# Four graph layers on one adjacency: VectorE's order in the attention layers written out, with small operations in lumps

## The chip, the cores and the metric

The kernel runs on one core of one Trainium2 chip. The metric is the device time of one execution in microseconds; a kernel's time is the median of its runs. All times below are microseconds.

## What is computed

A feature matrix x (4096 nodes, 64 features) passes through four layers over the same 0/1 adjacency matrix (4096 x 4096, float32). Each layer adds its result to x and normalizes the rows:

```python
x = _layernorm(x + _L0_gnn_ref(x, adj, L0_gnn_W, L0_gnn_b))
x = _layernorm(x + _L1_gnn_ref(x, adj, L1_gnn_r, L1_gnn_w_att, L1_gnn_b_att))
x = _layernorm(x + _L2_gnn_ref(x, adj, L2_gnn_weight, L2_gnn_bias))
x = _layernorm(x + _L3_gnn_ref(x, adj, L3_gnn_att_w, L3_gnn_att_b))
```

Layer 0 is a mean over neighbours, followed by a weight matrix, a relu and a normalization of rows. Layer 2 sums support rows (x times a weight matrix) over the last neighbours of a row, each weighted by a power of one half by its place in the row. Layers 1 and 3 are attention in hyperbolic space; their core is

```python
adj_att = sigmoid(left[:, None] + right[None, :] + b_att[0]) * adj
x_local = logmap(x[:, None, :], x[None, :, :], c)      # for every pair of nodes
support = einsum('ij,ijd->id', adj_att, x_local)
return proj(expmap(x, support, c), c)
```

where `left` and `right` are one number for each node. The pairwise `logmap` is not built as a 4096 x 4096 x 64 array: the kernel brings it to a function of one number z for each pair of nodes, and sums rows of features weighted by it.

## The kernel before, in words

**Staging.** The adjacency does not stay on the chip. Each layer streams it once, in 64 loads of 1 MB (`load`), into a pool of six buffers, all issued by the sync engine. The nodes on the output side form four groups of 1024 columns, taken in the order 3, 2, 1, 0 (`GROUPS`). For each group the 32 blocks of 128 source rows are taken two at a time, so that a layer has 4 x 16 = 64 pairs of blocks.

**An attention pass** (`attend`, L914 to L962). For each block of a pair, PE builds z (128 x 1024) in PSUM by three kinds of matmul (L935, L938, L941; z has two buffers), ScalarE (ACT) makes `sig`, the sigmoid (L943), and `sq`, a square of z (L946), and VectorE (DVE) makes t = max(z, 0) * sig (L949). After both blocks of the pair VectorE makes t = (sq + const) * t on 128 x 2048 (L951), and PE adds the pair to the sums `acc` of the group (L955). These three VectorE operations a pair, two L949 and one L951, are the large ones.

**The small work between.** When a group's pass is over, its sums are turned back to rows and go through `move` (L972 to L1072): about 90 VectorE operations, most on [128, 8] (one number for each of the group's 1024 nodes), a few on [128, 512] (all features of the group). It ends with the normalized rows of the next layer. `norm_rows` and `prepare` (with its part `second`) do the like for the rows that enter an attention: they build the operands of the z matmuls, and `left` and `right`. `linear` and `supports` make layer 2's support rows. The reciprocal square roots are `rsqrt` (L669): a first guess by integer arithmetic and three Newton steps (L677, L678, L679), each operation of which reads the one before it.

**What places the small work.** These parts are Python generators. `later` puts one into one of two queues, `tick(n)` advances a counter by n, and a queue's first generator runs to its next `yield` when its wait has passed; `yield n` asks for a wait of n ticks. `attend` calls `tick(rate)` behind each L949 and behind L951, where `rate` is given for each of the four groups. Three helpers give waits: `soon()`, `near()` and `after(small)`; `place[0]` says which layer runs. `need(tag)` ticks until a part is done.

**What sets the order on the engines.** The source gives one order; a scheduler then places instructions on each engine as it expects them to become ready. Layers 0 and 2 keep the source's order on PE and ACT (`FIXED`), and leave VectorE to the scheduler. In both attentions all engines are left to it. VectorE therefore often has one small operation between two large ones, whatever the source's order.

The functions that the change touches:

Of the kernel before, what the change touches and what calls it, by code (L numbers as in the profile page):

```python
# [21 lines left out]
D = 64  # L22
# [36 lines left out]
def gnn_stack_kernel(  # L59
# [509 lines left out]
    def stream(fits):  # L569

        with ExitStack() as st:
# [46 lines left out]
            def soon():  # L618


                return 0 if place[0] in (0, 2) else 1

            def after(small):


                each = {0: 1.6, 2: 6.0}.get(place[0])
                return 1 if each is None else 1 + int(small / each)

# [40 lines left out]
            def rsqrt(a, name):  # L669

                n = a.shape[1]
                r, t = nums(name, n), nums("rs_t", n)
                V.tensor_scalar(
                    r.bitcast(I32), a.bitcast(I32), -0.5, float(0x5F3759DF), ALU.mult, ALU.add
                )
                for _ in range(3):
                    V.tensor_mul(t, r, r)  # L677
                    V.scalar_tensor_tensor(t, t, -0.5, a, ALU.mult, ALU.mult)  # L678
                    V.scalar_tensor_tensor(r, t, 1.5, r, ALU.add, ALU.mult)  # L679
                return r  # L680

# [63 lines left out]
            def curved(c, name, least):  # L745


                c2, sc, rsc, of_y, root, short = (
                    num(keep, name + n, 1)
                    for n in ("_c2", "_sc", "_rsc", "_of_y", "_root", "_short")  # L750
                )
                V.tensor_scalar(c2, c, -2.0, None, ALU.mult)
                V.tensor_copy(rsc, rsqrt(c, "rsc"))
                V.tensor_mul(root, rsc, c)
                V.tensor_scalar(of_y, rsc, -((2.0 * UNIT) ** -0.5), None, ALU.mult)
                V.tensor_scalar(rsc, rsc, 0.996, None, ALU.mult)
                V.tensor_scalar(sc, root, -((2.0 * UNIT) ** 0.5), None, ALU.mult)
                V.tensor_scalar(short, root, least, None, ALU.mult)
                return c, c2, sc, rsc, of_y, root, short

            def norm_rows(layer, s, v, x2_to):

                m, v2, sq = nums("n_m"), nums("n_v2"), grp("sq")
                V.tensor_reduce(m, v, AX.X, ALU.add)
                V.tensor_scalar(m, m, 1.0 / D, None, ALU.mult)
                yield soon()
                V.tensor_sub(v, v, over(m))
                nc.gpsimd.tensor_mul(sq, v, v)
                yield soon()
                yield soon()  # L770
                V.tensor_reduce(v2, sq, AX.X, ALU.add)
                yield soon()
                V.tensor_scalar(m, v2, 1.0 / D, 1e-5, ALU.mult, ALU.add)
                r = rsqrt(m, "n_r")
                yield soon()
                V.tensor_mul(x_of(layer)[:, blocks(s), :], v, over(r))
                V.tensor_mul(x2_to, r, r)
                V.tensor_mul(x2_to, x2_to, v2)
                yield soon()

            def prepare(layer, s, att, b_att, curve, least, good, small):
# [6 lines left out]
                V.tensor_scalar(bg, cx2[:, at], -1.0, 1.0, ALU.mult, ALU.add)  # L788
                V.reciprocal(rbg, bg)

                V.tensor_scalar(rbg, rbg, -0.13, 0.0, ALU.max, ALU.min)
# [5 lines left out]
                def second():  # L797
# [12 lines left out]
                    for k, of in ((7, 0), (8, 0), (9, 1)):  # L810
                        nc.gpsimd.tensor_scalar(
                            ed[:, :, k], hl[:, :, of], -2.0 / UNIT, None, ALU.mult
                        )
                    V.tensor_sub(ys[:, :, D : 2 * D], y, ys[:, :, :D])

                    m, g, w = nums("m"), nums("g"), grp("xw")
                    V.tensor_scalar(g, cx2[:, at], 1.0, 1.0 / D, ALU.add, ALU.mult)
                    V.tensor_scalar(m, rbg, CUBE / UNIT, None, ALU.mult)
                    yield 1
                    V.tensor_add(w, xg, over(g))  # L820
                    yield 1
                    V.tensor_mul(xe[:, at, :], w, over(m))

                    q, q1, t = nums("q"), nums("q1"), nums("tt")
                    V.tensor_scalar(q, x2[:, at], least, c, ALU.max, ALU.mult)
                    V.tensor_scalar(q1, q, SMALL, None, ALU.max)
                    rt = rsqrt(q1, "rt")
                    V.tensor_mul(t, q1, rt)
# [32 lines left out]
                    V.tensor_scalar(m, bg, of_y, None, ALU.mult)  # L861
                    yield 1
                    lr, own = row.tile([P, WB, 2], F32, name="lr"), nums("own")
# [108 lines left out]
            def move(layer, s, sums, curve):  # L972
# [13 lines left out]
                held.pop()  # L986
                yield near()
                V.tensor_reduce(sum_1, of, AX.X, ALU.add)
# [5 lines left out]
                nc.scalar.activation(sq, u, AF.Square)  # L994
                yield near()
                yield soon()
                V.tensor_reduce(uu, sq, AX.X, ALU.add)
# [7 lines left out]
                V.tensor_mul(kx, k, x2g)  # L1005
                V.scalar_tensor_tensor(t2, d, -2.0, kx, ALU.mult, ALU.add)
                V.tensor_mul(t2, t2, k)
                V.tensor_add(t2, t2, uu)
# [5 lines left out]
                un, r_un = nums("un"), nums("r_un")  # L1014
                V.scalar_tensor_tensor(un, t2, root, rsqrt(t2, "r_t2"), ALU.mult, ALU.mult)
                V.tensor_scalar(un, un, fac, short, ALU.mult, ALU.max)
# [3 lines left out]
                nc.scalar.activation(th, un, AF.Tanh, scale=lam)  # L1020
                yield near()
                V.scalar_tensor_tensor(un, r_un, fac, th, ALU.mult, ALU.mult)
# [9 lines left out]
                V.tensor_add(y2, xy, y2)  # L1032
                V.tensor_add(den, den, xy)
                V.tensor_sub(p, y2, p)
                V.tensor_scalar(den, den, 1e-15, None, ALU.max)
# [8 lines left out]
                V.tensor_mul(t, q, q)  # L1044
                V.scalar_tensor_tensor(w2, qd, 2.0, px, ALU.mult, ALU.add)
                V.tensor_mul(t, t, uu)
                V.tensor_mul(w2, w2, p)
# [3 lines left out]
                yield soon()  # L1051
                n = rsqrt(t, "n")
                V.tensor_scalar(n, n, rsc, 1.0, ALU.mult, ALU.min)
# [8 lines left out]
                V.tensor_scalar(w2, w2, 1.0 / D, 1e-5, ALU.mult, ALU.add)  # L1062
                r = rsqrt(w2, "n")
                V.scalar_tensor_tensor(p, p, 1.0, r, ALU.add, ALU.mult)
# [3 lines left out]
                V.tensor_mul(u, u, over(q))  # L1068
                yield soon()
                yield soon()  # L1070
                V.tensor_add(x_of(layer + 1)[:, at, :], u, w)
                yield after(72)  # L1072

            def linear(layer, s, weights, finish):

                for h in range(2):
# [18 lines left out]
                    yield near()  # L1095
                    finish(slice(s * WB + h * SB, s * WB + (h + 1) * SB), t)
                    held.pop()
                    yield 1

            def supports(at, t):  # L1100

                nc.scalar.activation(halves[:, at, :D], t, AF.Copy, scale=SUP)
                V.scalar_tensor_tensor(
                    halves[:, at, D:], t, SUP, halves[:, at, :D], ALU.mult, ALU.subtract
                )
# [21 lines left out]
            with ExitStack() as lp:  # L1127
# [45 lines left out]
                def own_part(at, t):  # L1173

                    V.tensor_add(xw[:, at, :], t, b0_sb[:, None, :].to_broadcast([P, SB, D]))

                def end_0(s, tops):
# [3 lines left out]
                    for top, low in tops:  # L1181
                        t = take(F32, P, SB, P)
                        for k in range(SB):
                            cols = slice(k * P, (k + 1) * P)
                            to = t[:, k, : D + 1]
                            nc.tensor.matmul(to, top[:, cols], sum_w, start=True, stop=False)
                            nc.tensor.matmul(to, low[:, cols], count_w, start=False, stop=True)
                        ts.append(t)
                    for h, t in enumerate(ts):
                        at = slice(s * WB + h * SB, s * WB + (h + 1) * SB)  # L1190
# [4 lines left out]
                        V.tensor_add(zz, zz, xw[:, at, :])  # L1195
                    held.clear()
                    V.tensor_scalar(z, z, 0.0, None, ALU.max)
                    sq, n2 = grp("sq"), nums("n2")
                    nc.gpsimd.tensor_mul(sq, z, z)
                    yield 1  # L1200
                    V.tensor_reduce(n2, sq, AX.X, ALU.add)
                    V.tensor_scalar(n2, n2, 1e-24, None, ALU.max)
                    n = rsqrt(n2, "n")
                    yield 1
# [8 lines left out]
                with tc.manual_schedule(engines=FIXED):  # L1213
                    for s in GROUPS:
# [42 lines left out]
                        if s > 0:  # L1257
                            own_of = linear(0, s - 1, w0_sb[:D, :], own_part)
                            later(in_turn((0, s - 1), own_of))


# [19 lines left out]


            attention(1, curve1, (2, 1, 1, 1), lambda s: linear(2, s, w2_sb, supports))


            place[0] = 2

            def end_2(s, sums):
# [3 lines left out]
                t = to_rows_of(sums)  # L1292
                yield 1
                V.scalar_tensor_tensor(
# [84 lines left out]

            attention(3, curve3, (4, 1, 1, 1), store)  # L1380

# [84 lines left out]
```

## Time and profile before

| | us |
|---|---|
| median of 3 runs | 1155.24 (1150.9 to 1157.15) |
| profiled execution | 1151.7 |
| its span in the profile | 1150.0 |
| PE busy in the span | 1019.8 (89%) |
| VectorE busy in the span | 960.8 (84%) |
| ACT busy in the span | 812.2 (71%) |
| POOL busy in the span | 60.9 (5%) |

The layers follow one another; in the profiled execution layer 0 runs to 192.7, attention 1 to 528.4, layer 2 to 768.0, attention 3 to 1112.6, and the last group's move and the stores to 1150.0.

The rows of the profile for the attention's inner operations, both attentions together (busy us and mean ns of one, then idle time of the engine ahead of them and what ended most of it):

```
L943 ACT ACTIVATE sig<-left_b,right 128x1024 f32<-128x1024 f32 x256 | 293.8, 1149 | 44.8 <-DVE t L949 33.7
L949 DVE SCALAR_TENSOR_TENSOR t<-z,sig 128x1024 f32<-128x1024 f32 x256 | 309.8, 1215 | 15.5 <-ACT sq L946 14.6
L946 ACT ACTIVATE sq<-z,turn 128x1024 f32<-128x1024 f32 x256 | 281.4, 1105 | 30.2 <-PE z L941 27.9
L951 DVE SCALAR_TENSOR_TENSOR t<-sq,t 128x2048 f32<-128x2048 f32 x128 | 292.9, 2288 | 0.7
L955 PE MATMUL acc<-t,xe 128*64 128x512 f32 x1024 | 260.3, 622 | 33.5 <-DVE t L951 30.0
```

A matmul's duration includes the time that it overlaps with its neighbours, and so does that of a VectorE operation to a smaller part: the distance from one start to the next is what an operation takes on a busy engine.

### The profile page before, as it was taken

What the parts mean: (1) busy time and instruction counts of PE and PEld (TensorE: products, weight loads), DVE (VectorE), ACT (ScalarE), POOL (GpSimd) and SP (SyncE); (2) the same over time, 40 slices, a digit from 0 to 9 for tenths busy, and PEclk for the clock granted to TensorE, in tenths of its full rate; (3) what the DMA queues carried; (4) which work ended last, traced back from release to release, by engine and by line L of the source; (5) the groups of instructions that cost most, each with busy time, mean ns of one, the idle gap of its engine ahead of it and who ended that gap; (6) DMA issues with size and microseconds to landing.
All of it is one profiled execution on the core that took longest, in us unless ns stands there. A gap on an engine that the chain in (4) does not pass through costs nothing.

```text
span 1150.0 us, 13516 instructions
## 1 busy us (share of the span) xinstructions
PE 1019.8 (89%) x4917; PEld 389.6 (34%) x4917; DVE 960.8 (84%) x1901; ACT 812.2 (71%) x823; POOL 60.9 (5%) x97
## 2 busy tenths in 40 slices
PE   6889997899899999988999997998788999899970
PEld 3445554233333333332333232332323333233220
DVE  7587888989999899989773584249988999999996
ACT  0003215899889799976767688777997999889860
POOL 0020120000000000000000020001100000000001
PEclk9998998999999999999999999999998999999995
DMA  9999898546456455643988886695354655555400
GB/s 352 421 385 412 358 390 337 199 158 217 180 214 220 156 214 215 220 160 141 323 300 310 314 308 255 227 358 193 110 183 155 223 213 215 210 211 212 154 0 22
DMA packets 38418, 271.57 MB, mean 236 GB/s; under 512 B 4550, under 2 KB 4550, under 8 KB 5574
## 3 DMA queue, kind: packets, MB, share of 16 engines
q1 hardware_dynamic: 37440, 269.50, 63.0%
q10 hardware_dynamic: 902, 1.12, 0.3%
q8 instruction: 40, 0.66, 0.2%
q14 instruction: 36, 0.29, 0.1%
HBM read 269.55 MB, written 1.05 MB: 235 GB/s over the span
## 4 chain that ended last, share of the span: by engine, by line
DVE 54%; PE 30%; ACT 6%; DMA 5%; issue 2%; POOL 2%; ACTq 0%; POOLq 0%; SPq 0%; DVEq 0%
DVE t L951 21%; DVE t L949 21%; PE z L1340 9%; PE acc L1356 5%; PE acc L1229 5%; DMA edges<-in_adj_dram 5%; PE acc L955 3%; ACT sq L946 2%; ACT sq L1349 1%; PE aux L1092 1%; PE z L935 1%; PE aux L842 1%; ACT sig L943 1%; PE z L938 1%; DVE junk L741 1%
## 5 line engine op out<-in xcount | busy, mean ns | idle before, releaser
L943 ACT ACTIVATE sig<-left_b,right 128x1024 f32<-128x1024 f32 x256 | 293.8, 1149 | 44.8 <-DVE t L949 33.7
L949 DVE SCALAR_TENSOR_TENSOR t<-z,sig 128x1024 f32<-128x1024 f32 x256 | 309.8, 1215 | 15.5 <-ACT sq L946 14.6
L946 ACT ACTIVATE sq<-z,turn 128x1024 f32<-128x1024 f32 x256 | 281.4, 1105 | 30.2 <-PE z L941 27.9
L951 DVE SCALAR_TENSOR_TENSOR t<-sq,t 128x2048 f32<-128x2048 f32 x128 | 292.9, 2288 | 0.7
L955 PE MATMUL acc<-t,xe 128*64 128x512 f32 x1024 | 260.3, 622 | 33.5 <-DVE t L951 30.0
L935 PE MATMUL z<-edges,two_i 128*128 128x512 bf16 x512 | 202.7, 396 | 20.5 <-DVE t L949 20.3
L941 PE MATMUL z<-dst,src 74*128 74x512 f16 x512 | 196.2, 383 | 0.0
L938 PE MATMUL z<-lo_hi,hi_lo 128*128 128x512 f16 x512 | 195.4, 382 | 0.0
L1349 ACT ACTIVATE sq<-z,at_edge 128x1024 bf16<-128x1024 f32 x128 | 141.8, 1113 | 57.0 <-PE z L1340 56.1
L955 PEld LDWEIGHTS acc<-t,xe 128*64 128x64 f32 x1024 | 64.2, 139 | 171.3 <-DVE t L951 89.3
L741 DVE SCALAR_TENSOR_TENSOR t<-edges 128x2048 bf16<-128x2048 f32 x32 | 73.7, 2312 | 47.1 <-DMA edges<-in_adj_dram 46.2
L1229 PE MATMUL acc<-edges,first 128*128 128x512 bf16 x256 | 82.5, 404 | 19.4 <-DMA edges<-in_adj_dram 19.4
L935 PEld LDWEIGHTS <-two_i 128*128 128x128 bf16 x512 | 50.5, 99 | 141.6 <-issue 97.7
L1356 PE MATMUL acc<-sq,halves 128*64 128x512 bf16 x512 | 80.1, 393 | 16.8 <-ACT sq L1349 16.1
L1229 PE MATMUL acc<-edges,third 128*65 128x512 bf16 x256 | 81.8, 402 | 0.0
L741 DVE SCALAR_TENSOR_TENSOR junk<-edges 128x2048 bf16<-128x2048 f32 x32 | 73.1, 2285 | 7.8 <-DMA edges<-in_adj_dram 7.5
L1340 PE MATMUL z<-edges,enter 128*128 128x512 bf16 x256 | 78.9, 390 | 0.0
L1340 PE MATMUL z<-edges,pass_by 128*128 128x512 bf16 x248 | 77.8, 394 | 0.0
L938 PEld LDWEIGHTS <-hi_lo 128*128 128x128 f16 x512 | 50.5, 99 | 69.4 <-issue 25.8
L941 PEld LDWEIGHTS <-src 74*128 74x128 f16 x512 | 49.6, 97 | 69.3 <-issue 5.1
L1356 PEld LDWEIGHTS <-halves 128*64 128x64 f16 x512 | 19.2, 108 | 73.9 <-issue 73.8
L1229 PEld LDWEIGHTS <-first 128*128 128x128 bf16 x256 | 24.4, 100 | 48.1 <-issue 21.0
(260 smaller groups left out, 758.9 us busy)
## 6 DMA issues: line engine op xcount, KB each, us to landing
edges<-in_adj_dram SPq DMA_DIRECT2D x256, 1024.0 KB, 5.6
x<-in_x_dram SPq DMA_DIRECT2D x4, 256.0 KB
out_dram<-x ACTq DMA_DIRECT2D x4, 256.0 KB, 4.2
w_sb<-in_L_gnn_W_dram ACTq DMA_DIRECT2D x1, 32.0 KB, 4.7
given<-in_L_gnn_b_dram ACTq DMA_DIRECT2D x1, 0.2 KB
given<-in_L_gnn_bias_dram ACTq DMA_DIRECT2D x1, 0.2 KB
given<-in_L_gnn_b_att_dram ACTq DMA_DIRECT2D x1, 0.0 KB
given<-in_L_gnn_att_b_dram ACTq DMA_DIRECT2D x1, 0.0 KB
```

Source lines behind the costliest of these rows:

```text
L741: V.scalar_tensor_tensor(junk, a, 0.0, a, ALU.not_equal, ALU.not_equal, accum_out=odd[:, n : n + 1])
L935: nc.tensor.matmul(half, two_i, edge[:, at : at + W], start=True, stop=False)
L938: nc.tensor.matmul(half, hi_lo[:, of], lo_hi[:, to], start=False, stop=False)
L941: nc.tensor.matmul(half, src[:, of], dst[:, to], start=False, stop=True)
L943: nc.scalar.activation(sig, left_b, AF.Sigmoid, bias=right[:, j : j + 1])
L946: nc.scalar.activation(sq[:, k], zp, AF.Square, bias=turn, scale=-1.0 / UNIT)
L949: V.scalar_tensor_tensor(t[:, k], zp, 0.0, sig, ALU.max, ALU.mult)
L951: V.scalar_tensor_tensor(t, sq, HIGH**2, t, ALU.add, ALU.mult)
L955: nc.tensor.matmul(acc[h * D : (h + 1) * D, :], xe[:, j, :], t[:, k, h * W : (h + 1) * W], start=j == BLOCKS[0], stop=j == BLOCKS[-1],)
L1229: nc.tensor.matmul(accs[h][:m], lhs[:, j, :], edge[:, at : at + W], start=j == BLOCKS[0], stop=j == BLOCKS[-1],)
L1340: nc.tensor.matmul(z[:, h : h + W], lhs, rhs[:, h : h + W], start=j == BLOCKS[0], stop=True, skip_group_check=True,)
L1356: nc.tensor.matmul(acc[0][h * D : (h + 1) * D, :], halves[:, j, part * D : (part + 1) * D], w[:, h * W : (h + 1) * W], start=j == BLOCKS[0 ...
```

## The change

Both calls of `attention` now stand in a block that gives VectorE the source's order; PE, ACT and POOL are still left to the scheduler there. Around it the waits of the small work are written anew:

- `rsqrt` is a generator that yields `soon()` behind its first and its second Newton step, so that a step's three operations stand together. Each root has a scratch tile of its own name.
- A new wait `back()`, three ticks in an attention, stands ahead of VectorE operations that read what another engine has made. Behind the copy of L985 there are six ticks.
- `after()` is 0 in an attention, where it was 1.
- Further `yield soon()` cut long stretches in `move` and `prepare`, and the subtraction into `ys` is moved behind the product into `xe`.
- Layer 0's last group must have its sums read (`need((0, 0, "sums"))`) before attention 1 begins.
- Attention 3 ticks at rates (2, 1, 1, 1), before (4, 1, 1, 1).

What is computed, and the count of VectorE's operations, is unchanged. The diff, cut to its core:

```diff
+            def back():
+                return near() if place[0] in (0, 2) else 3
             def after(small):
                 each = {0: 1.6, 2: 6.0}.get(place[0])
-                return 1 if each is None else 1 + int(small / each)
+                return 0 if each is None else 1 + int(small / each)
...
             def rsqrt(a, name):
-                r, t = nums(name, n), nums("rs_t", n)
+                r, t = nums(name, n), nums(name + "_t", n)
...
-                for _ in range(3):
+                for n in range(3):
                     V.tensor_mul(t, r, r)
                     V.scalar_tensor_tensor(t, t, -0.5, a, ALU.mult, ALU.mult)
                     V.scalar_tensor_tensor(r, t, 1.5, r, ALU.add, ALU.mult)
+                    if n < 2:
+                        yield soon()
...
             def norm_rows(layer, s, v, x2_to):
                 nc.gpsimd.tensor_mul(sq, v, v)
-                yield soon()
-                yield soon()
+                yield back()
                 V.tensor_reduce(v2, sq, AX.X, ALU.add)
...
-                r = rsqrt(m, "n_r")
+                r = yield from rsqrt(m, "n_r")
...
             def prepare(layer, s, att, b_att, curve, least, good, small):
-                    V.tensor_sub(ys[:, :, D : 2 * D], y, ys[:, :, :D])
+                    yield soon()
...
                     V.tensor_mul(xe[:, at, :], w, over(m))
+                    yield soon()
+                    V.tensor_sub(ys[:, :, D : 2 * D], y, ys[:, :, :D])
...
             def move(layer, s, sums, curve):
                 nc.scalar.copy(of.rearrange("p (h k) f -> p h k f", h=2), t)
                 held.pop()
-                yield near()
+                yield near() if place[0] == 2 else 6
                 V.tensor_reduce(sum_1, of, AX.X, ALU.add)
...
                 nc.scalar.activation(sq, u, AF.Square)
-                yield near()
-                yield soon()
+                yield back()
                 V.tensor_reduce(uu, sq, AX.X, ALU.add)
...
                 V.scalar_tensor_tensor(t2, d, -2.0, kx, ALU.mult, ALU.add)
+                yield soon()
                 V.tensor_mul(t2, t2, k)
...
             def end_0(s, tops):
                         ts.append(t)
+                    yield soon() * 4
...
                     held.clear()
+                    done.add((0, s, "sums"))
...
+                    need((0, 0, "sums"))
...
-            attention(1, curve1, (2, 1, 1, 1), lambda s: linear(2, s, w2_sb, supports))
+            with tc.manual_schedule(engines={mybir.EngineType.DVE}):
+                attention(1, curve1, (2, 1, 1, 1), lambda s: linear(2, s, w2_sb, supports))
...
-            attention(3, curve3, (4, 1, 1, 1), store)
+            with tc.manual_schedule(engines={mybir.EngineType.DVE}):
+                attention(3, curve3, (2, 1, 1, 1), store)
+            place[0] = 4
```

More of the change, by code (lines that the diff above doesn't have):

```diff
@@ L752, in curved @@
                 V.tensor_scalar(c2, c, -2.0, None, ALU.mult)
-                V.tensor_copy(rsc, rsqrt(c, "rsc"))
+                of_c = rsqrt(c, "rsc")
+                while True:
+                    try:
+                        next(of_c)
+                    except StopIteration as last:
+                        V.tensor_copy(rsc, last.value)
+                        break
                 V.tensor_mul(root, rsc, c)
@@ L818, in second @@
                     V.tensor_scalar(m, rbg, CUBE / UNIT, None, ALU.mult)
-                    yield 1
                     V.tensor_add(w, xg, over(g))
-                    yield 1
+                    yield soon()
                     V.tensor_mul(xe[:, at, :], w, over(m))
+                    yield soon()
+                    V.tensor_sub(ys[:, :, D : 2 * D], y, ys[:, :, :D])
                     q, q1, t = nums("q"), nums("q1"), nums("tt")
@@ L826, in second @@
                     V.tensor_scalar(q1, q, SMALL, None, ALU.max)
-                    rt = rsqrt(q1, "rt")
+                    rt = yield from rsqrt(q1, "rt")
                     V.tensor_mul(t, q1, rt)
@@ L861, in second @@
                     V.tensor_scalar(m, bg, of_y, None, ALU.mult)
-                    yield 1
+                    yield back()
                     lr, own = row.tile([P, WB, 2], F32, name="lr"), nums("own")
@@ L994, in move @@
                 nc.scalar.activation(sq, u, AF.Square)
-                yield near()
-                yield soon()
+                yield back()
                 V.tensor_reduce(uu, sq, AX.X, ALU.add)
@@ L1006, in move @@
                 V.scalar_tensor_tensor(t2, d, -2.0, kx, ALU.mult, ALU.add)
+                yield soon()
                 V.tensor_mul(t2, t2, k)
@@ L1014, in move @@
                 un, r_un = nums("un"), nums("r_un")
-                V.scalar_tensor_tensor(un, t2, root, rsqrt(t2, "r_t2"), ALU.mult, ALU.mult)
+                r_t2 = yield from rsqrt(t2, "r_t2")
+                V.scalar_tensor_tensor(un, t2, root, r_t2, ALU.mult, ALU.mult)
                 V.tensor_scalar(un, un, fac, short, ALU.mult, ALU.max)
@@ L1020, in move @@
                 nc.scalar.activation(th, un, AF.Tanh, scale=lam)
-                yield near()
+                yield back()
                 V.scalar_tensor_tensor(un, r_un, fac, th, ALU.mult, ALU.mult)
@@ L1033, in move @@
                 V.tensor_add(den, den, xy)
+                yield soon()
                 V.tensor_sub(p, y2, p)
@@ L1045, in move @@
                 V.scalar_tensor_tensor(w2, qd, 2.0, px, ALU.mult, ALU.add)
+                yield soon()
                 V.tensor_mul(t, t, uu)
@@ L1051, in move @@
                 yield soon()
-                n = rsqrt(t, "n")
+                n = yield from rsqrt(t, "n")
                 V.tensor_scalar(n, n, rsc, 1.0, ALU.mult, ALU.min)
@@ L1062, in move @@
                 V.tensor_scalar(w2, w2, 1.0 / D, 1e-5, ALU.mult, ALU.add)
-                r = rsqrt(w2, "n")
+                r = yield from rsqrt(w2, "n_2")
                 V.scalar_tensor_tensor(p, p, 1.0, r, ALU.add, ALU.mult)
@@ L1068, in move @@
                 V.tensor_mul(u, u, over(q))
-                yield soon()
-                yield soon()
+                yield back()
                 V.tensor_add(x_of(layer + 1)[:, at, :], u, w)
@@ L1095, in linear @@
                     yield near()
-                    finish(slice(s * WB + h * SB, s * WB + (h + 1) * SB), t)
+                    yield from finish(slice(s * WB + h * SB, s * WB + (h + 1) * SB), t)
                     held.pop()
@@ L1102, in supports @@
                 nc.scalar.activation(halves[:, at, :D], t, AF.Copy, scale=SUP)
+                yield back()
                 V.scalar_tensor_tensor(
@@ L1175, in own_part @@
                     V.tensor_add(xw[:, at, :], t, b0_sb[:, None, :].to_broadcast([P, SB, D]))
+                    yield 0
                 def end_0(s, tops):
@@ L1199, in end_0 @@
                     nc.gpsimd.tensor_mul(sq, z, z)
-                    yield 1
+                    yield back()
                     V.tensor_reduce(n2, sq, AX.X, ALU.add)
                     V.tensor_scalar(n2, n2, 1e-24, None, ALU.max)
-                    n = rsqrt(n2, "n")
+                    n = yield from rsqrt(n2, "n")
                     yield 1
@@ L1292, in end_2 @@
                 t = to_rows_of(sums)
-                yield 1
+                yield back()
                 V.scalar_tensor_tensor(
```

## The prediction, made before the changed kernel ran

> **What bounds the kernel now.** I read the chain of waits first, then the busy times by stage (cut at the first and last L949 or L951 of each attention), then VectorE's timeline inside a stage. The chain, and the stages (columns: window, its length, busy us of PE, PE's weight loads, DVE, ACT, POOL with instructions, granted clock, DMA share, GB/s):
>
> ```profile
> DVE 54%; PE 30%; ACT 6%; DMA 5%; issue 2%; POOL 2%; ACTq 0%; POOLq 0%; SPq 0%; DVEq 0%
> ...
> 192.70:528.40 335.70, 313.34 (x1367) 111.70 (x1367) 319.46 (x442) 293.25 (x288) 9.11 (x13) 0.98 0.55 197
> 528.40:768.00 239.60, 222.72 (x1205) 73.64 (x1203) 133.38 (x360) 177.34 (x180) 11.72 (x19) 0.99 0.78 281
> 768.00:1112.60 344.60, 313.26 (x1385) 109.58 (x1383) 334.19 (x519) 301.35 (x294) 13.24 (x21) 0.98 0.51 183
> 1112.60:1150.00 37.40, 2.87 (x13) 0.98 (x13) 26.52 (x144) 2.22 (x5) 4.38 (x3) 0.60 0.05 17
> ```
>
> In both attentions VectorE is busy 95 to 97% of the time, PE 91 to 93%; in layer 2 (second line) VectorE has 44% to spare. Over the whole run PE is the busiest engine, but in the stages that change VectorE is. The reader is to see that VectorE's own length sets an attention, and that layer 2 could take small operations free of charge.
>
> What a small operation costs stands in the timeline (start, duration, engine, line):
>
> ```profile
> 206.83 2.29 DVE L951 SCALAR_TENSOR_TENSOR t<-sq,t 128x2048 f32<-128x2048 f32 x1
> 209.04 0.16 DVE L678 SCALAR_TENSOR_TENSOR rs_t<-rs_t,n_m 128x8 f32<-128x8 f32 x1
> 209.12 1.22 DVE L949 SCALAR_TENSOR_TENSOR t<-z,sig 128x1024 f32<-128x1024 f32 x1
> 210.25 0.15 DVE L679 SCALAR_TENSOR_TENSOR n_r<-rs_t,n_r 128x8 f32<-128x8 f32 x1
> 210.32 1.22 DVE L949 SCALAR_TENSOR_TENSOR t<-z,sig 128x1024 f32<-128x1024 f32 x1
> 211.46 0.15 DVE L677 TENSOR_TENSOR rs_t<-n_r 128x8 f32<-128x8 f32 x1
> 211.57 2.29 DVE L951 SCALAR_TENSOR_TENSOR t<-sq,t 128x2048 f32<-128x2048 f32 x1
> ...
> 240.37 0.17 DVE L871 SCALAR_TENSOR_TENSOR f<-f,q 128x8 f32<-128x8 f32 x1
> 240.57 0.17 DVE L872 TENSOR_TENSOR f<-f,m 128x8 f32<-128x8 f32 x1
> 240.77 0.17 DVE L874 TENSOR_TENSOR left<-lr,f 128x8 f32<-128x8 f32 x1
> 240.86 0.16 DVE L875 TENSOR_TENSOR right<-lr,f 128x8 f32<-128x8 f32 x1
> ...
> 250.00 2.29 DVE L951 SCALAR_TENSOR_TENSOR t<-sq,t 128x2048 f32<-128x2048 f32 x1
> 252.30 2.55 DVE L949 SCALAR_TENSOR_TENSOR t<-z,sig 128x1024 f32<-128x1024 f32 x2
> 254.88 2.29 DVE L951 SCALAR_TENSOR_TENSOR t<-sq,t 128x2048 f32<-128x2048 f32 x1
> ```
>
> Durations overlap, so starts are the price. A [128,8] operation costs 0.08 when the next operation does not read its result (209.04 to 209.12; 874 to 875), and 0.20 when it does (871, 872): a premium of 0.12. The scheduler puts one step of the Newton chain behind each large operation, so that the large one covers the premium. The same view gives 1.13 for L949, 2.21 for L951 (0.12 more for an L951 directly behind the L949 whose t it reads), about 0.60 for a 512-wide operation. A pair of blocks is 2 x 1.13 + 2.21 = 4.47 on VectorE; bare pairs follow each other at 4.88 here, at 4.62 to 4.86 in a long row of them: 4.74 on average, which I take as the floor that PE and ACT set.
>
> Around the ends of passes VectorE does wait, which the change is aimed at (brackets: idle before, releaser):
>
> ```profile
> 396.18 1.23 DVE L949 SCALAR_TENSOR_TENSOR t<-z,sig 128x1024 f32<-128x1024 f32 x1 [2.37 <-ACT sq L946]
> ...
> 401.79 0.69 DVE L999 TENSOR_REDUCE d<-w_att 128x8 f32<-128x512 f32 x1 [1.45 <-POOL w_att L992]
> ```
>
> **What the Trainium skill says.** "Vector Engine (DVE) Microarchitecture Reference", section "5.2 Measured stream behaviour on trn2", gives about 1.04 ns a column and 75 ns an instruction: 0.083, 1.14 and 2.21 us for 8, 1024 and 2048 columns. The trace agrees (0.08, 1.13, 2.21). "VectorE: DVE Perf Modes", section "The DRAIN you can't avoid", says to minimize the count of operations, not the semaphores between them. The trace disagrees for tiny ones: a reader directly behind costs 0.20 against 0.08. My prediction rests on that measured difference.
>
> **The change, part by part.** The order of the built programs shows that VectorE now follows the source exactly and has as many instructions as before (1839 in the order). Three things move: small operations stand in lumps of three to five dependent ones, waits are longer in ticks, and more small work falls into the attentions.
>
> *Attention pairs.* I summed the 63 pair cycles of each attention, from one L951 to the next, with the prices above, each pair at least 4.74. Per attention (1 before, 1 after, 3 before, 3 after):
> - large operations, 63 x 4.47: 281.6 in all four
> - [128,8] operations x 0.08: 226, 306, 289, 345 of them: 18.1, 24.5, 23.1, 27.6
> - their readers directly behind x 0.12: 8, 168, 6, 195: 1.0, 20.2, 0.7, 23.4
> - L951 directly behind L949 x 0.12: 11, 34, 8, 35: 1.3, 4.1, 1.0, 4.2
> - 512-wide (23, 27, 32, 36) and others: 18.1, 20.9, 20.3, 24.3
> - pairs lifted to the floor (37, 25, 37, 25): 3.4, 3.8, 2.1, 3.8
>
> Sums 323.5, 355.1, 328.8, 364.9. From the timeline the 63 cycles of before took 339.1 (196.20 to 535.32) and 341.1 (771.56 to 1112.63). So before waited 15.6 and 12.3 beyond its sum. Where it is only busy, the sum is close: pairs that hold 5.35 and 8.71 of priced work took 5.44 and 8.87.
>
> What of the waits goes? The source's order puts readers of another engine three to six ticks behind (L985 to L988, L992 to L999), so most. I keep 2.5 in attention 1, where three casts, four copies and two table loads stand between two sq on ACT (some 16 us of ACT against 9.5 of VectorE plus its lead), and 2 in attention 3. Its two further table loads (21 against 19) at 1.28 each in the trace are 2.6 on ACT, with 13% of ACT idle there: nothing to 2.6, I take nothing. Attention 1: 355.1 + 2.5 - 339.1 = +18.5, and +0.4 for its first pair. Attention 3: 364.9 + 2 - 341.1 = +25.8.
>
> *Layers 0 and 2.* Some 60 small operations leave layer 2, where VectorE is 56% busy, so nothing is won; its first L949 no longer waits for L1294: -0.5. PE keeps a written order there, with a few aux groups moved: 0, bounds -3 to +3. The sums of group 0 drained at the end of layer 0 lie behind DMA (share 0.95 there): 0, bounds 0 to 1.
>
> *POOL, SP and ACT queues.* POOL's 97 instructions keep their kinds and lie under large VectorE work; the 256 loads of SP keep their order, and their start is freed by PE. Nothing, unless the pairs stretch.
>
> *The end.* When the last pass is over, before still has the move of the group ahead of it to do:
>
> ```profile
> 1112.63 2.28 DVE L951 SCALAR_TENSOR_TENSOR t<-sq,t 128x2048 f32<-128x2048 f32 x1
> ...
> 1119.27 0.68 DVE L988 TENSOR_REDUCE sum<-z 128x8 f32<-128x512 f32 x1
> ...
> 1126.88 0.69 DVE L991 TENSOR_TENSOR u<-z,k 128x512 f32<-128x512 f32 x1
> ```
>
> With rate 2 that move is done earlier: 87 VectorE operations follow the last L951, not 145. L991 comes 0.9 behind L988, at 1120.2: -6.7. The rest of the last chain is dependent in both.
>
> Sum: 18.5 + 0.4 + 25.8 - 0.5 - 6.7 = +37.5. Operations that read a result two places back start 0.12 apart, not 0.08 (1116.46 to 1116.58 in the tail): +1 to +2 over the lumps. Total +39, and the profiled span of 1150.0 becomes 1189. The profiled execution took 1151.7, 1.7 more than its span, and lies 3.5 below the median of 1155.2; so 1194 against the median.
>
> **Rivals.** *F, the forecast, 0.76:* lumps on a bound VectorE cost their premium, +39, 1194; its own range 1182 to 1206 comes from the tail at half (+3), the skew of waits (0 to 8 kept instead of 4.5) and the premium 0.09 to 0.14 (-11 to +7).
>
> *B, 0.12:* the lumps also hold up z's two buffers, so that PE and ACT stop and restart in every pair above the floor. In the waits of attention 1, ACT's sig already waits for L949 34 times, up to 1.4; 38 + 38 such pairs by 0.5 (half a sq) are +38: 1232. Against it: before's own crowded pairs exceed their sum by only 0.1 to 0.2.
>
> *C, 0.05:* premiums are partly hidden, a lump falling where VectorE would have waited for sq anyway. At 0.04 instead of 0.12 the 349 further readers cost 28 less: 1166. For it: 25 pairs keep slack. Against it: they are in the sum already.
>
> *D, the other side, 0.07:* PE is the bound after all (89% busy overall against 84%), the lumps lie under it, and only gains stay: waits 27.9 - 4.5, the end 6.7, the gap 0.5, so -30: 1125. It decides once the premium falls under 0.12 - 39/349 = 0.01, in other words if dependent operations cost nothing more. The 240.37 lines, inside an attention, speak against it. Halfway cases give the chance of no change.
>
> That the change does not do what it says is excluded by the order of the build.
>
> **Numbers.** This measurement can tell about 0.5% (5.8 us) from no change. Predicted 1194. Range 1164 to 1220: all of F with some more waits, and C; B and D, 0.19, are left out. Faster 0.05, same 0.03, slower 0.92.
>
> **What would show it.** Right: an attention of 355 to 370 by its 63 cycles with VectorE busy 97% or more, PE's share falling, lump operations 0.20 apart, hardly any idle before L988 and L999, a last stage of about 31. Wrong: L949 waiting for sq or z behind a lump (B), cycles with full lumps near 5 us (C, D), or a last stage that still holds two moves.

## The result, and the profile after

The changed kernel takes 1215.63 us (median of 4 runs, 1211.44 to 1217.14), before 1154.35 beside it: a ratio of 1.0527, with a 95% interval of 1.0487 to 1.0566. It is slower by 61 us; 1194 was predicted, inside a range of 1164 to 1220; the result lies 4 us from that range's upper end, and above the 1182 to 1206 that the prediction gave its main case. The profiled execution took 1216.02, with a span of 1214.3, 64.3 more than the span before.

First the chain of waits of the changed kernel, from its page:

```profile
DVE 48%; PE 34%; ACT 10%; DMA 5%; issue 2%; POOL 1%; ACTq 0%; SPq 0%; POOLq 0%; DVEq 0%
```

VectorE still leads it, but PE and ACT have grown. Next, the busy times by stage of the changed kernel: attention 1 from its first L961 (the old L949) to the end of its last L963 (the old L951), layer 2, attention 3 and the end. The columns are as in the prediction.

```profile
189.60:566.80 377.20, 322.01 (x1372) 114.20 (x1395) 357.82 (x543) 299.22 (x295) 17.45 (x14) 0.96 0.53 181
566.80:797.40 230.60, 215.55 (x1154) 71.82 (x1176) 114.54 (x289) 170.75 (x173) 11.37 (x18) 0.97 0.80 286
797.40:1182.20 384.80, 319.86 (x1362) 111.64 (x1382) 360.53 (x578) 303.01 (x296) 12.28 (x22) 0.96 0.48 164
1182.20:1214.30 32.10, 4.39 (x13) 1.38 (x13) 17.62 (x86) 2.01 (x4) 2.83 (x2) 0.55 0.03 11
```

The windows of before in the prediction ended attention 1 at 528.4, when its last L951 but one had just begun. With the same cuts as above, before reads:

```profile
192.70:537.60 344.90, 320.48 (x1396) 113.87 (x1395) 328.67 (x453) 299.95 (x293) 9.11 (x13) 0.98 0.54 196
537.60:768.00 230.40, 215.57 (x1175) 71.47 (x1175) 124.18 (x350) 170.64 (x174) 11.72 (x19) 0.99 0.79 286
```

So layer 2 took the same 230 us with 10 us less of VectorE work in it, and both attentions grew, by 32 and 40 us. VectorE's busy time there rose by 29 and 26; the share in which it is busy did not rise, as I had said it would (to 97% or more), but fell to 94 to 95%. PE's share did fall as forecast, from 93 and 91% to 85 and 83%.

From L963 to L963, as the prediction counts, the 63 cycles took 369.5 and 381.9 us, against 339.1 and 341.1. That is +30.4 and +40.8. Attention 1 lies in the 355 to 370 that the prediction named as a sign of being right, attention 3 does not. The end is 5.3 shorter, the stretch between the attentions 0.4 shorter, and the first L963 came 1.2 earlier: together +64.3.

What a lump costs is seen in VectorE's timeline of the changed kernel:

```profile
1031.94 0.16 DVE L676 TENSOR_SCALAR r_t<-t 128x8 int32<-128x8 int32 x1
1032.13 0.17 DVE L680 TENSOR_TENSOR r_t_t<-r_t 128x8 f32<-128x8 f32 x1
1032.34 0.17 DVE L681 SCALAR_TENSOR_TENSOR r_t_t<-r_t_t,t 128x8 f32<-128x8 f32 x1
1032.54 0.17 DVE L682 SCALAR_TENSOR_TENSOR r_t<-r_t_t,r_t 128x8 f32<-128x8 f32 x1
1032.62 2.28 DVE L963 SCALAR_TENSOR_TENSOR t<-sq,t 128x2048 f32<-128x2048 f32 x1
1034.82 0.16 DVE L680 TENSOR_TENSOR r_t_t<-r_t 128x8 f32<-128x8 f32 x1
1035.02 0.17 DVE L681 SCALAR_TENSOR_TENSOR r_t_t<-r_t_t,t 128x8 f32<-128x8 f32 x1
1035.22 0.17 DVE L682 SCALAR_TENSOR_TENSOR r_t<-r_t_t,r_t 128x8 f32<-128x8 f32 x1
1035.30 1.22 DVE L961 SCALAR_TENSOR_TENSOR t<-z,sig 128x1024 f32<-128x1024 f32 x1
```

The starts of operations that read the one ahead are 0.19 to 0.21 apart; the last of a lump, which the large operation does not read, takes 0.08. With the prediction's prices for each operation in its place, the two attentions sum to 354.8 and 364.8 (the prediction's rounded terms gave 355.1 and 364.9). In pairs with 7 to 12 small operations the mean is 6.04 by price and 6.11 by the trace in attention 1, and 6.24 against 6.27 in attention 3. The prices hold. What did not come as forecast is the rest: 14.7 and 17.1 us beyond the sums.

A large part of that rest stands at the starts of passes. VectorE in the changed kernel, where pair 80 of 128 (counted from 0) begins a pass:

```profile
910.76 2.29 DVE L963 SCALAR_TENSOR_TENSOR t<-sq,t 128x2048 f32<-128x2048 f32 x1
913.80 1.22 DVE L961 SCALAR_TENSOR_TENSOR t<-z,sig 128x1024 f32<-128x1024 f32 x1 [0.74 <-ACT sq L958]
917.24 1.23 DVE L961 SCALAR_TENSOR_TENSOR t<-z,sig 128x1024 f32<-128x1024 f32 x1 [2.22 <-ACT sq L958]
918.50 2.29 DVE L963 SCALAR_TENSOR_TENSOR t<-sq,t 128x2048 f32<-128x2048 f32 x1
```

This cycle holds no small operation at all, is priced 4.59, and took 7.74. Before had the same stretch at pair 80, and used it:

```profile
870.88 2.29 DVE L951 SCALAR_TENSOR_TENSOR t<-sq,t 128x2048 f32<-128x2048 f32 x1
873.09 0.68 DVE L988 TENSOR_REDUCE sum<-z 128x8 f32<-128x512 f32 x1
873.80 0.17 DVE L989 TENSOR_SCALAR k<-sum 128x8 f32<-128x8 f32 x1
873.92 1.22 DVE L949 SCALAR_TENSOR_TENSOR t<-z,sig 128x1024 f32<-128x1024 f32 x1
875.06 0.68 DVE L991 TENSOR_TENSOR u<-z,k 128x512 f32<-128x512 f32 x1
877.13 0.69 DVE L999 TENSOR_REDUCE d<-w_att 128x8 f32<-128x512 f32 x1 [1.39 <-POOL w_att L992]
```

Here the first operations of the move lie beside ACT's and PE's lateness: seven small operations of 2.9 us, and the next L951 at 879.92, 9.04 after the last. In the changed kernel they come later and are paid for in pairs of their own.

### The profile page after: what moved, and what is told of

Read it like the earlier page. It is cut to its first block, busy times and chain, and to the rows that moved or that the text cites. A ratio compares the mean times of both kernels' runs of the same rounds, so it can differ in the third digit from the quotient of the medians.

```text
span 1214.3 us, 13417 instructions
## 1 busy us (share of the span) xinstructions
PE 1024.5 (84%) x4831; PEld 390.7 (32%) x4917; DVE 994.0 (82%) x1901; ACT 811.5 (67%) x825; POOL 68.7 (6%) x97
## 4 chain that ended last, share of the span: by engine, by line
DVE 48%; PE 34%; ACT 10%; DMA 5%; issue 2%; POOL 1%; ACTq 0%; SPq 0%; POOLq 0%; DVEq 0%
DVE t L963 16%; DVE t L961 14%; PE z L1360 10%; PE acc L967 6%; PE acc L1376 6%; DMA edges<-in_adj_dram 4%; ACT sq L958 4%; PE z L947 3%; PE z L950 3%; PE z L953 2%; DVE junk L746 2%; ACT sig L955 2%; PE acc L1247 1%; ACT sq L1369 1%; POOL sq L779 1%
## 5 line engine op out<-in xcount | busy, mean ns | idle before, releaser
L961 DVE SCALAR_TENSOR_TENSOR t<-z,sig 128x1024 f32<-128x1024 f32 x256 | 308.7, 1218 | 44.6 <-ACT sq L958 42.2
L967 PE MATMUL acc<-t,xe 128*64 128x512 f32 x1024 | 264.1, 639 | 83.6 <-DVE t L963 83.3
L963 DVE SCALAR_TENSOR_TENSOR t<-sq,t 128x2048 f32<-128x2048 f32 x128 | 292.9, 2288 | 2.4
L947 PE MATMUL z<-edges,two_i 128*128 128x512 bf16 x463 | 184.0, 397 | 33.0 <-DVE t L961 31.4
L1247 PE MATMUL acc<-edges,first 128*128 128x512 bf16 x241 | 76.3, 393 | 19.5 <-DMA edges<-in_adj_dram 19.1
```

The lines of the kernel that those rows point to most:

```text
L947: nc.tensor.matmul(half, two_i, edge[:, at : at + W], start=True, stop=False)
L961: V.scalar_tensor_tensor(t[:, k], zp, 0.0, sig, ALU.max, ALU.mult)
L963: V.scalar_tensor_tensor(t, sq, HIGH**2, t, ALU.add, ALU.mult)
L967: nc.tensor.matmul(acc[h * D : (h + 1) * D, :], xe[:, j, :], t[:, k, h * W : (h + 1) * W], start=j == BLOCKS[0], stop=j == BLOCKS[-1],)
L1247: nc.tensor.matmul(accs[h][:m], lhs[:, j, :], edge[:, at : at + W], start=j == BLOCKS[0], stop=j == BLOCKS[-1],)
```

## The experiments

All times are medians; each kernel ran beside the kernel before (1151.2 to 1152.9 in these comparisons), and the ratio is to that. "The changed kernel" is 1215.63, measured beside 1154.35, so a difference of 2 or 3 us between two comparisons says nothing; where it matters the ratios are compared. Line numbers are those of each kernel, and shift with its edit.

**1. The new waits without the written order.** The block around each attention is taken away, all else of the change stays:

```diff
-            with tc.manual_schedule(engines={mybir.EngineType.DVE}):
-                attention(1, curve1, (2, 1, 1, 1), lambda s: linear(2, s, w2_sb, supports))
+            attention(1, curve1, (2, 1, 1, 1), lambda s: linear(2, s, w2_sb, supports))
```

(and the same for attention 3)

> The changed kernel with its new waits, roots and rates, but VectorE's order in the attentions left to the scheduler again. By the price list its pairs sum to 324.1 and 329.1 in the two attentions (before 323.2 and 328.9, after 354.8 and 364.8). Theory P (operations placed directly behind the one they read, and more small work in the attentions, are what costs): back near before, 1145 to 1165 us. Rival Y (the new, longer waits themselves move small work out of the stretches where VectorE is idle, whoever orders it): stays above 1185. If the longer waits remove waiting, as I forecast, under 1140.

It took 1144.95, ratio 0.9935 (0.9921 to 0.9948): faster than both kernels. Its cycles took 338.8 and 333.3, so 14.7 and 4.2 beyond the sums; the end took 38.9. So, with the new waits in the source, the written order alone turns a small gain of 0.65% into the loss. It makes the cycles 79.3 longer: 66.4 by the priced sums and 12.9 by waits, all of these in attention 3; it takes 6.8 off the end. The rewritten waits and rates do go with less waiting in attention 3 (12.2 before, 4.2 here), as long as the scheduler may place the operations; the other parts of the gain, such as a first L963 4.2 earlier, I did not separate. The written order with the old waits was not run.

**2. Shorter waits, the written order kept.**

```diff
-                return near() if place[0] in (0, 2) else 3
+                return near() if place[0] in (0, 2) else 1
...
-                yield near() if place[0] == 2 else 6
+                yield near()
```

> The changed kernel with one tick instead of three ahead of readers of other engines, and one tick instead of six behind the copy of z0. Its priced sum hardly moves (356.3 and 364.5 against 354.8 and 364.8). Theory H (the idle stretches at the start of a pass are made by ACT and PE, and the six ticks carry the move's first operations past them): those operations fall into the stretches again, 8 to 20 us faster than the changed kernel, 1196 to 1208, with less idle ahead of the first L961s of a pass. Rival: VectorE then waits ahead of the readers instead, and the time is the same or longer, 1213 to 1235.

1213.93, ratio 1.0536 (1.0491 to 1.0581). Theory H's 8 to 20 us did not come. The operations did move back to the start of the pass, but in a fixed order VectorE takes them and then still waits (at pair 16, from the trace of this kernel):

```profile
294.62 0.68 DVE L1000 TENSOR_REDUCE sum<-z 128x8 f32<-128x512 f32 x1
295.33 0.17 DVE L1001 TENSOR_SCALAR k<-sum 128x8 f32<-128x8 f32 x1
295.44 1.23 DVE L961 SCALAR_TENSOR_TENSOR t<-z,sig 128x1024 f32<-128x1024 f32 x1
296.58 0.68 DVE L1003 TENSOR_TENSOR u<-z,k 128x512 f32<-128x512 f32 x1
299.40 1.23 DVE L961 SCALAR_TENSOR_TENSOR t<-z,sig 128x1024 f32<-128x1024 f32 x1 [2.14 <-ACT sq L958]
```

The theory is not wholly wrong: the waits at pairs 16, 80, 96 and 112 fell from 11.9 to 8.7, and the cycles of attention 3 from 381.9 to 377.1. The stretch between the attentions was 3.0 longer in this trace, and the whole time is the same.

**3. The same lumps, not dependent.** In the attentions, each Newton step becomes three operations on the argument:

```diff
+                    if place[0] in (1, 3):
+                        for m in range(3):
+                            V.scalar_tensor_tensor(
+                                nums(f"{name}_t{m}", a.shape[1]), a, -0.5, a, ALU.mult, ALU.mult
+                            )
+                        if n < 2:
+                            yield soon()
+                        continue
```

> The changed kernel, with the Newton steps of the attentions' roots done at the same places and in the same number, but each on the root's argument with a scratch tile of its own, so that none reads the one before it; the roots themselves are the first guess. 92 and 106 of the 174 and 203 readers directly behind are gone, all else in the order is the same. Theory P (0.12 us for each): sums 343.8 and 352.0, so -11.0 and -12.8, and about 3 in the last chain: 27 less than the changed kernel, 1189. If the premium is hidden behind other engines: 1210 to 1217.

The whole time, 6449 us, says nothing: in this run the kernel's general path followed the four layers (its matmuls fill the trace after 1200 us). The attentions ahead of it can be read: 356.5 and 368.6, against 369.5 and 381.9. That is -13.0 and -13.3, where the 0.12 a reader gave -11.0 and -12.8. A Newton step in its timeline:

```profile
1011.48 0.31 DVE L682 SCALAR_TENSOR_TENSOR r_t_t<-t 128x8 f32<-128x8 f32 x3
1011.71 2.28 DVE L971 SCALAR_TENSOR_TENSOR t<-sq,t 128x2048 f32<-128x2048 f32 x1
```

Three operations at the same place take 0.23 here, and 0.48 in the changed kernel (1034.82 to 1035.30).

**4 and 5. Four more operations behind each L963, apart or chained.**

```diff
+                    for n in range(4):                                  # apart
+                        V.tensor_scalar(nums(f"more{n}"), right[:, blocks(GROUPS[0])], 0.5, None, ALU.mult)
...
+                    more = nums("more")                                 # chained
+                    V.tensor_scalar(more, right[:, blocks(GROUPS[0])], 0.5, None, ALU.mult)
+                    for _ in range(3):
+                        V.tensor_scalar(more, more, 0.5, None, ALU.mult)
```

> The changed kernel with four more [128, 8] operations behind each L963 of both attentions (512 in all), none reading another. Price list at 0.08 each, less the slack of the pairs at the floor: sums +16.5 and +15.7, about 1248 us. Rival B (a lump keeps z's two buffers from PE and ACT, half a microsecond of restart in a pair): 1275 or more.

> The same four operations at the same places, each reading the one before it: 3 of 4 at 0.20. Price list: sums +39.2 and +38.4 over the changed kernel, about 1293 us, so 45 more than with the four apart. If the order in which the operations depend on each other is hidden by other engines, the same as the four apart.

Apart: 1233.64, ratio 1.0709 (1.0672 to 1.0745). Chained: 1276.39, ratio 1.108 (1.1042 to 1.1118). First apart, then chained:

```profile
971.41 0.38 DVE L965 TENSOR_SCALAR more<-right 128x8 f32<-128x8 f32 x4
971.70 0.16 DVE L1063 TENSOR_TENSOR mt<-mt,uu 128x8 f32<-128x8 f32 x1
```

```profile
1008.27 0.16 DVE L965 TENSOR_SCALAR more<-right 128x8 f32<-128x8 f32 x1
1008.47 0.58 DVE L967 TENSOR_SCALAR more<-more 128x8 f32<-128x8 f32 x3
1008.96 0.16 DVE L680 TENSOR_TENSOR n_t<-n 128x8 f32<-128x8 f32 x1
```

Four apart take 0.29, four chained 0.69. The attentions together took 771.5 and 815.3: 43.8 for the chaining, against 45.4 by price. 128 x 3 = 384 readers by 42.75 us of medians is 0.11 each. Rival B falls: with four more in every pair the pairs did not stretch beyond their sum. On the contrary, the time rose by 18, not by the 32 of the sum, because the waits of attention 3 fell from 17.1 to 5.9. That pointed to the next question, what makes those waits.

**6 and 7. A third buffer for sig**, in the changed kernel and in the kernel of experiment 1:

```diff
-                        sig = sb.tile([P, WW], F32, name="sig")
+                        sig = sb.tile([P, WW], F32, name="sig", bufs=3)
```

> The changed kernel with a third buffer for sig; VectorE's order is the same to the instruction. Theory H2: the some 32 us beyond the priced sums that are left in the attentions come from ACT, which runs one sigmoid ahead, then waits for L961 to free a sig buffer while the next sq is late (2.2 us idle at most starts of a pass): 5 to 12 us faster than the changed kernel, 1203 to 1211, with less idle ahead of L961. Rival: what is late is PE's z or the copies on ACT, and a third sig buffer changes nothing: 1212 to 1218.

> The kernel with the new waits and VectorE left to the scheduler (1145 us), with a third buffer for sig. H2: 3 to 8 us faster than without, 1137 to 1142, and faster than the kernel before by 1% or more. Rival: 1142 to 1150.

1218.42 (ratio 1.0581, 1.0545 to 1.0618) and 1152.69 (1.0007, 0.9991 to 1.0024). H2 falls: in the first of them the idle stretch at the start of pair 80 is 0.74 and 2.22, as without. The second kernel is even 8 us longer than experiment 1 although VectorE's sums agree to 0.2 and the cycles of attention 1 to 0.4. In the profiled executions attention 3 took 338.8 against 333.3 and the stretch between the attentions 244.9 against 237.1. These traces overstate the difference: they are of an execution of 1157.64, 5 above its median, and of one of 1141.79, 3 below its median, and the granted clock in layer 2 was 0.96 in the one and 0.99 in the other. Part of attention 3's 5.5 stands at pair 73, where PE's order here holds z matmuls back behind `acc` (the pattern of experiment 9) and in experiment 1 does not. The rest I did not find.

**8. The rate of attention 3.** `(2, 1, 1, 1)` set back to `(4, 1, 1, 1)` in the changed kernel.

> The changed kernel with attention 3's rates at (4, 1, 1, 1) again. My prediction put the shorter end down to the rate. In the build 85 operations follow the last L963 with either rate, so if VectorE's written order makes the end short, it stays at about 32 us here, and the time changes by the priced sum, 1.4 less: 1211 to 1217. If the rate makes it: an end near 37 and 1219 or more.

1219.71, ratio 1.0576 (1.053 to 1.0623). The total falls where the other case was expected, but the end, which tells the two apart, stays short: 32.3 (1191.34 to 1223.6). So the rate does not make it; the written order does, as the 38.9 of experiment 1, with rate 2 and no written order, says too. Attention 3 itself took 4.6 more, in waits; the granted clock there was 0.93, in the changed kernel 0.96, so how much of this comes from the rate is open.

**9. PE's order at the start of a pass.** At pair 80 of the changed kernel, PE does this, in this order:

```profile
913.02 0.38 PE L950 MATMUL z<-lo_hi,hi_lo 128*128 128x512 f16 x1
913.32 1.94 PE L967 MATMUL acc<-t,xe 128*64 128x512 f32 x8
915.20 0.39 PE L953 MATMUL z<-dst,src 74*128 74x512 f16 x1
```

The last z matmul of a block stands behind the `acc` matmuls of the pair ahead, which wait for that pair's L963 (910.76 to 913.05 in the lines shown above). So sq for that block can't start before 915.6 (it starts at 916.1, behind a sigmoid), and VectorE's second L961 waits until 917.2. In the build's order, and in the trace, exactly the pairs 16, 80, 96 and 112 have this, where four transposes of the move's sums (L981) stand among the z matmuls; in experiment 4 none of them has. One line of the changed kernel moves the transposes:

```diff
-                    later(move_s)
+                    later(move_s, False, 5)
```

> The changed kernel with each group's move starting five ticks later. In the build of the changed kernel PE's order has, at the start of pairs 16, 80, 96 and 112 of 128, four transposes of the move's sums among the next z's matmuls, and the last z matmul behind the acc matmuls of the pair ahead (11 z matmuls there in place of 12); these are the pairs with some 3 us of waiting. With the later move all pairs have 12. VectorE's priced sums stay (354.8 and 364.6). Theory Z (PE's order makes these waits): the waits of pairs 16, 80, 96 and 112 go, 8 to 11 us faster than the changed kernel, 1204 to 1208. Rival (the copies on ACT make them): they move with the copies and stay, 1212 to 1218.

1205.78, ratio 1.0467 (1.0444 to 1.049), so 10 less, or 7 by the ratios, much as theory Z says. At the start of pair 80 the wait is gone:

```profile
908.37 2.29 DVE L963 SCALAR_TENSOR_TENSOR t<-sq,t 128x2048 f32<-128x2048 f32 x1
910.92 2.36 DVE L961 SCALAR_TENSOR_TENSOR t<-z,sig 128x1024 f32<-128x1024 f32 x2 [0.26 <-ACT sq L958]
913.31 2.29 DVE L963 SCALAR_TENSOR_TENSOR t<-sq,t 128x2048 f32<-128x2048 f32 x1
```

The transposes and ACT's copy behind them are still there, a little later; but no z matmul stands behind `acc` any more. Attention 3 has 8.7 beyond its sum in place of 17.1. Attention 1 gained only 0.6; as the wait of pair 16 went, one beside ACT's copies and table loads (pair 4) grew from 2.4 to 3.5, and the rest is spread.

**10 and 11. The same in the kernel of experiment 1**, with five ticks and with three:

> The kernel with the new waits and VectorE left to the scheduler (1145 us), with the move five ticks later. Sums 319.5 and 327.6 (324.1 and 329.1 without), 11 z matmuls at no pair in place of pairs 16 and 80, so by P and Z 5 to 10 us faster: 1135 to 1140. Rival: the work only goes to the end or to layer 2, 1143 to 1150.

> The same with three ticks: sums 319.1 and 329.0, PE's order at pairs 16 and 80 as it was, but not the split at pair 39. By P and Z 4 to 8 us faster than without: 1137 to 1141. Rival: 1143 to 1150.

1145.66 (ratio 0.9957, 0.994 to 0.9973) and 1146.77 (0.9958, 0.9944 to 0.9972): no gain over 1144.95. Attention 1 took 4.4 and 4.6 less, attention 3 0.8 and 3.4 more, the stretch between them 242.0 and 240.4 in place of 237.1, and the end 41.5 and 39.8 in place of 38.9. That is what the rival said. The traces can't settle how much of the stretch is the edit's: the granted clock in layer 2 was 0.96 in both, and 0.99 in that of experiment 1. At pairs 16 and 80 experiment 1 already had 3.6 us of other work in the hole that PE's order makes, and 1.4 of waiting was left at each, so there was little to win.

The lowest median is that of experiment 1, 0.65% under the kernel before; that is clear of its own interval, but those of experiments 10 and 11 overlap with it.

## Why the prediction was right, and where its sum was short

- **Lumps cost their premium: right.** In the sum the readers directly behind and the close L963 were +19.2 + 2.8 in attention 1 and +22.7 + 3.2 in attention 3. Experiment 3 took 24 of it by price out, and 26.3 went; experiment 5 against 4 gives 0.11 a reader.
- **More small work in the attentions: right in the sum.** It is 80 and 56 more [128, 8] operations and 4 more 512-wide ones in each. VectorE has some 60 operations fewer in layer 2, as many fewer in the end, and some 30 fewer in layer 0. Layer 2 gave nothing back for it: 230.4 before, 230.6 after.
- **The waits that were to go: wrong, and the mis-sized term.** The prediction kept 4.5 of the 27.9 us that before waited beyond its sums. Measured are 31.8 (14.7 and 17.1). That is 27.3 of difference, against 25 by which the whole span was under-forecast; the other terms nearly cancel. What was kept came as said: pairs 4 and 72, beside ACT's copies and the table loads of the Ln, have 4.6. What the sum did not have at all is PE's order: pairs 16, 80, 96 and 112 cost 11.9 us by it (experiment 9). The other 15 are spread over many pairs, none above 1.7, and their cause stays open. I had read the waits at the ends of passes as VectorE standing at a small operation that came too early, which more ticks in a fixed order would cure. The waits for POOL's w_att did go: 8.6 us in 6 cases before (L999), 1.4 in one case after. The ticks alone did not do it, for experiment 1 has 7.7 in 6 cases. But such waits were the smaller part, and the two lines of before that the prediction shows as its evidence (396.18 and 401.79) lie in holes that PE makes. The L949 at 396.18 waits for a sq whose z comes late, behind 16 matmuls of the next layer's `linear` (389.35 to 392.5 in PE's timeline). For the second line PE has this:

```profile
395.06 0.38 PE L938 MATMUL z<-lo_hi,hi_lo 128*128 128x512 f16 x1
...
397.99 1.93 PE L955 MATMUL acc<-t,xe 128*64 128x512 f32 x6
399.86 0.39 PE L941 MATMUL z<-dst,src 74*128 74x512 f16 x1
```

The last z matmul stands behind `acc` here too, so that the next L949 could not have started before 402.1, whether L999 waited or not. In before, z matmuls stand behind `acc` in this way at pairs 16, 37, 58 and 80, and the cycles there have some 12 of its 27.9 us. A fixed order on VectorE can't remove such holes; it only takes away what lay in them.

- **The end: right in size, wrong in cause.** 5.3 came of the 6.7. L1003 follows L1000 by 0.98, as said, but L1000 itself came 7.70 behind the last L963, before 6.64. I put it down to the rate; experiment 8 shows that it is the written order.
- **Operations two places apart (+1 to +2): not seen** as a separate term; the crowded pairs agree with the sum to 0.1.
- **The gap (-0.5), the first pair (+0.4):** -0.4 and -1.2; both lie within what those stretches differ between kernels (the first L963 came at 192.0 to 196.2 in the traces here).
- **Rivals.** B, restarts in every crowded pair, is excluded by experiment 4. Its sign came all the same: inside the cycles the idle time ahead of L961 is 24.3 us, before 15.5 (ahead of L949); but most of it stands in pairs with three small operations or fewer, not behind lumps. C and D, hidden premiums, are excluded by experiments 3 and 5.
- **The range.** That 1215.63 fell inside it is in part luck: the main case counted on 0 to 8 us of waits and the range on "some more"; 31.8 came, in good part by a cause that the prediction did not have.
- **The Trainium skill.** "VectorE: DVE Perf Modes", section "Rules for kernel authors", advises for chained operations to lower their count, not the number of semaphores. For [128, 8] the count alone does not give the price here: four operations take 0.29 or 0.69 by whether they read each other.

## What to carry to other kernels

On an engine that bounds a stage, price small operations by the distance between starts, and price a reader directly behind its producer apart; an order that puts one step of a chain behind each long operation hides that premium, one that groups the steps pays it. Before an order is fixed on the engine that waits, look for who makes the wait: if another engine's order does, the fixed order loses what used to fill the hole and keeps the hole. Here the scheduler, given the same waits in the source, beat the written order by 71 us.

## What the runs showed that I had not expected

One matmul in the wrong place of PE's order cost about 3 us of VectorE, where the matmul itself takes 0.2: it stood behind eight others that wait for VectorE's last large operation and then take 1.9 us. And more work on VectorE (512 operations apart) cost 18 us in place of 32: in that kernel no z matmul stands behind `acc` at the four pairs. Why the scheduler placed PE's work differently there is not shown.
